# A decoder's second layer: two batches' sums of expert results as small parts of their own, and the queries' rotation in two pieces

## The chip, the core and the metric

The kernel runs on one core of a Trainium2 chip. The metric is the time on the device in microseconds, the median of the runs. A core has a matmul engine (TensorE, here PE), a vector engine (VectorE, DVE), a scalar engine (ScalarE, ACT), a general one (GpSimd, POOL) and a queue for transfers (SyncE, SP). Each engine works through its own list of instructions in order and waits for the others by semaphores.

## The reference, cut to what matters

Everything is float32. Four batches (b) of 256 tokens with 256 features go through two layers, each with three blocks, and every block ends with a residual sum and a layer norm:

```python
x = ln(x + attn0(x))                 # layer 0
x = ln(x + state_space(ctx, x))
x = ln(x + experts(x))               # 64 experts, the best 6 of each token, and a shared one
x = ln(x + linear_attention(x))      # layer 1
x = ln(x + cross_attention(x, ctx))  # 32 heads of 8, queries and keys rotated by position
x = ln(x + squared_relu_mlp(x))      # hidden size 1024, rounded to 255 steps of its row's maximum
```

The second layer's blocks start from the weighted sum of the six expert results of a token: `x += w[j] * y[j]`, j from 0 to 5, ahead of the third norm.

## The kernel before

`Net.l0` computes the first layer and leaves the expert results as rows in device memory (`ys`). `Net.tail` computes the rest, and only it concerns us. The 1024 tokens are eight tiles of 128 rows; batch b has the tiles 2b and 2b+1.

The order of the work in `tail` is written by hand, by means of generators. A `Part` wraps a generator; `go()` runs it to its next `yield`, `to(n)` until n yields are done, and `over` says that it has ended. Between two yields stands a piece. No instruction moves on an engine after that: what a piece issues stands in each engine's list in the order of the calls. The parts are, for each batch b:

- `linear(b)`: the sums of the expert results (`sums`, line 1317: one multiply-add of 128x256 on DVE for each of six results of each of two tiles; the results come as tiles `got` by DMA, three buffers, the next load issued by `load_got` after a tile's last product), moments and norm, `turn` (transposition `xtp` to `xT`), then linear attention (`q1p`, `kv1p`, `kvp`, `o1p`, `project` with `prt` and `prp`, a norm, another `turn`).
- `keys(b)` and `queries(b)`: the projection (`kv2p`, `q2p`), a copy to `raw` by ACT, the rotation `rope` into `pad`, and four pieces that each transpose a quarter (`pt`) and copy it to `kT` or `qT`. In `rope` POOL forms two products for each of the two tiles, and four more operations a tile run on DVE (on POOL for keys with b > 0). In `queries` and in `turned` a few matmuls into a scratch bank (`idle`) stand ahead of the first transposition.
- `output(b, oT)`: transpositions `pto`, division by the sums, `project`, norm and `turn`.
- `squared(b, i)`, one for each tile: `ph`, relu by ACT and square by POOL (`hr`); maximum (`xm`, line 1478), and scaling and rounding of `hr` (lines 1482 and 1483) by DVE; transpositions `fpt`; `fpo`, residual and moments; norm and the output's DMA.

The backbone is a loop over k from 0 to 37. Step k computes logits twice: `lgq` for the head group s = k % 8 of batch k // 8, with queries on the partitions, of which DVE takes the maximum (line 1430), and five steps later (`LAG`) `lgk` of the same group, with keys on the partitions, of which ACT takes the exponential (line 1434); `values` multiplies these with the values (`po`, line 1438). The maxima of four steps are transposed (`pm`) by `place`, and their negatives go by DMA as a row into `qT`, which `lgk` reads (`qT<-mxT`). Each step has two halves, and after each half the loop calls `fill(k, n)`, which lets up to n parts run one piece, three from step 5 on:

```python
now = [e for e in todo if not e[0].over and e[1](k)]
now = sorted(now, key=lambda e: e[0] not in soon)[:n]
```

Each entry of `todo` is a part with a condition (`may`): `lin[b]` may run when `lin[b - 1]` is over, `qs[b]` when `lin[b]` and `ks[b]` are over and its rows of the buffer are free, the parts of `sq` once `outs[b]` is over, in an order fixed by the yields that their predecessors have made. At the start of each batch's steps the loop forces what that batch needs (`lin[b].to(99)`, `ks[b].to(99)`, `qs[b].to(3 + s // 2)`).

All short-lived matmul results but `lgk` and `po`, that is `lgq`, `pt`, `xtp`, `q1p` and so on, share one tag of four PSUM banks that are handed out in turn (`bank`). So the n-th of them waits until the (n-4)-th has been read.

Of the kernel before, what the change touches and what calls it, by code (L numbers as in the profile page):

```python
# [61 lines left out]
class Net:  # L62
# [1102 lines left out]
    def tail(self):  # L1165
# [10 lines left out]
        nc, tc = self.nc, self.tc  # L1176
        H, HD, HP, K, NH, LAG = 32, 8, 32, self.K6, 1024, 5
        SCALE = float(np.float32(1.0) / np.sqrt(np.float32(HD)))
        w = self.w
        with ExitStack() as ctx:  # L1180
# [36 lines left out]
            def rope(b, raw, eng):  # L1217

                r = raw.rearrange("p t (h f i) -> p t h f i", h=H, i=2)
                dst = pad[:, :, :, 0:HD].rearrange("p t h (f i) -> p t h f i", i=2)  # L1220
                tmp = p1.tile([P, 2, 2, H, 4], F32, name="rtmp")
                for t in range(2):
                    cs = slice(8 * b + 4 * t, 8 * b + 4 * t + 4)
                    cos, sin = (v[:, cs].unsqueeze(1).to_broadcast([P, H, 4]) for v in self.trig)
                    x1, x2 = r[:, t, :, :, 0], r[:, t, :, :, 1]
                    d1, d2 = dst[:, t, :, :, 0], dst[:, t, :, :, 1]
                    nc.gpsimd.tensor_mul(tmp[:, t, 0], x2, sin)
                    nc.gpsimd.tensor_mul(tmp[:, t, 1], x2, cos)
                    eng.tensor_mul(d1, x1, cos)
                    eng.tensor_mul(d2, x1, sin)  # L1230
                    eng.tensor_sub(d1, d1, tmp[:, t, 0])
                    eng.tensor_add(d2, d2, tmp[:, t, 1])

            def turned(dst, g, n=0):

# [10 lines left out]
            def keys(b):  # L1246
                raw = p1.tile([P, 2, D], F32, name="raw")
                for t in range(2):
                    ps = bank("kv2p", 2 * D)
                    l0 = b * S + t * P  # L1250
                    self.mm(ps, [(w["ctxT"][:, 0, l0:l0 + P], w["wkv2"][:, 0, :])])
                    nc.scalar.copy(raw[:, t, :], ps[:, :D])
                    nc.scalar.copy(vps[b % 3][:, t, :, 0:HD], ps[:, D:].rearrange("p (h d) -> p h d", d=HD))
                yield
                rope(b, raw, nc.gpsimd if b else nc.vector)
                if b < 2:
                    clear(b + 1, nc.gpsimd)
                yield
                for g in range(4):
                    turned(kTs[b % 2], g, (8 if b == 0 else 3) if g == 0 else 0)  # L1260
                    yield

            def queries(b):
                raw = p1.tile([P, 2, D], F32, name="raw")
                ps = bank("q2p", 2, D)
                for t in range(2):
                    self.mm(ps[:, t, :], [(self.xT[b][:, k, t * P:(t + 1) * P], w["wq2"][:, k, :]) for k in range(KD)])
                nc.scalar.copy(raw, ps)
                yield
                rope(b, raw, nc.vector)  # L1270
                yield
                for g in range(4):
                    turned(qTs[b % 2], g, 5 if g == 0 else 0)
                    yield
# [34 lines left out]
                norm([2 * b, 2 * b + 1], res, mv)  # L1309
                yield  # L1310

            def sums(b):
                for i in range(2):
                    t = 2 * b + i
                    got = gots.pop(t)
                    for j in range(K):
                        nc.vector.scalar_tensor_tensor(  # L1317
                            self.x[t], got[:, j, :], self.wj[:, t, j:j + 1], self.x[t], ALU.mult, ALU.add
                        )
                        if b < 2 and j == 2:  # L1320
                            yield
                    load_got()
                    if i == 0:
                        yield
                res = [self.x[2 * b + i] for i in range(2)]
                mv = self.ln_moments(res)
                yield
                norm([2 * b, 2 * b + 1], res, mv)
                yield
# [136 lines left out]
            def squared(b, i):  # L1466
                t = 2 * b + i
                h = p3.tile([P, NH], F32, tag="g", name="hr")
                for n in range(2):
                    sl = slice(n * 512, n * 512 + 512)  # L1470
                    ph = bank("ph", 512)
                    self.mm(ph, [(self.xT[b][:, k, i * P:(i + 1) * P], w["cfc"][:, k, sl]) for k in range(KD)])
                    nc.scalar.activation(h[:, sl], ph, AF.Relu)  # L1473
                    nc.gpsimd.tensor_mul(h[:, sl], h[:, sl], h[:, sl])  # L1474
                yield
                xm = self.small.tile([P, 1], F32, name="xm")
                iv = self.small.tile([P, 1], F32, name="xiv")
                nc.vector.tensor_reduce(xm, h, AX.X, ALU.max)
                nc.vector.tensor_scalar(xm, xm, EPS, None, ALU.max)
                nc.vector.reciprocal(iv, xm)  # L1480

                nc.vector.tensor_scalar(h, h, iv, 255.0, ALU.mult, ALU.mult)
                nc.vector.tensor_scalar(h, h, MAGIC, MAGIC, ALU.add, ALU.subtract)
                nc.vector.tensor_scalar(xm, xm, 1.0 / 255.0, None, ALU.mult)
                yield
                hT = p3.tile([P, NH // P, P], F32, tag="g", name="hT")
                for q in range(0, NH // P, 4):
                    pt = bank("fpt", 4, P)
                    self.idle(pt[:, 0, :], 4 if t > 5 and q == 0 else 0)
                    for j in range(4):  # L1490
                        nc.tensor.transpose(pt[:, j, :], h[:, (q + j) * P:(q + j + 1) * P], self.ident)
                    nc.scalar.copy(hT[:, q:q + 4, :], pt)
                yield
                po = bank("fpo", D)
                self.mm(po, [(hT[:, j, :], w["cpj"][:, j, :]) for j in range(NH // P)])
                r = p2.tile([P, D], F32, name="rf")
                nc.vector.scalar_tensor_tensor(r, po, xm, self.x[t], ALU.mult, ALU.add)
                mv = self.ln_moments([r])
                yield
                norm([t], [r], mv)  # L1500
                nc.sync.dma_start(out=self.out[t * P:(t + 1) * P, :], in_=self.x[t])
                yield


            ks, qs, lin = ([Part(f(b)) for b in range(B)] for f in (keys, queries, linear))
            sq = [Part(squared(t // 2, t % 2)) for t in range(NT)]
            outs = [None] * B
            ks[0].to(99)
            self.exp_and_log()
            lin[0].to(4)  # L1510
            ks[1].to(2)
            lin[0].to(6)
# [1 line left out]
            first, second, k = lin[0], lin[1], ks[1]  # L1514
            for part in (
                second, second, first, second, first, k, first, k, first, first, second, first, k, second, first,
                second, k, first, second, first, second, first, second, first, qs[0], second, qs[0], second, qs[0],
            ):
                part.go()
            assert first.n == 17, first.n  # L1520
            first.to(99)
            ks[1].to(99)
            qs[0].to(3)

            def may(b):

                def rows(n, k):
                    return b < 2 or k >= 8 * (b - 2) + (3 + 2 * n if n > 1 else 6)  # L1530

                yield lin[b], lambda k: b == 0 or lin[b - 1].over
                yield ks[b], lambda k: b == 0 or (qs[b - 1].over and rows(ks[b].n, k))
                yield qs[b], lambda k: lin[b].over and ks[b].over and rows(qs[b].n, k)
                for i in range(2):
                    p, t = sq[2 * b + i], 2 * b + i
                    yield p, lambda k, p=p, t=t: (
                        outs[b] and outs[b].over and lin[-1].n > 1 and (t < 1 or sq[t - 1].n)
                        and (t < 2 or sq[t - 2].over) and (b == 0 or sq[2 * b - 1].n > (2 if p.n < 2 else 4))
                    )  # L1540

            todo = [e for b in range(B) for e in may(b)]

            def fill(k, n):

                soon = [p[min(k // 8 + 1, B - 1)] for p in (lin, ks, qs)]
                now = [e for e in todo if not e[0].over and e[1](k)]
                now = sorted(now, key=lambda e: e[0] not in soon)[:n]
# [7 lines left out]
            for k in range(8 * B + LAG + 1):  # L1556
                mt = divmod(k, 8) if k < 8 * B else None
                wt = divmod(k - LAG, 8) if 0 <= k - LAG < 8 * B else None
                if mt:
                    b, s = mt  # L1560
                    if s == 0:
                        lin[b].to(99)
                        ks[b].to(99)
                        mxs[b] = p2.tile([P, 2, 2, 16], F32, name="mx2")
                    qs[b].to(3 + s // 2)
                ws = [None] * 4
                for i in range(2):
                    half(i, wt, mt, ws)
# [152 lines left out]
```

## Time and profile before

| | before |
|---|---|
| median of 3 runs | 1191.1 us (1188.24 to 1193.07) |
| profiled execution: its own time | 1182.05 us |
| its span, first to last instruction | 1179.9 us |
| mean granted PE clock | 0.945 |
| PE busy | 1041.2 us (88%), 6340 matmuls |
| PE's weight loads | 764.2 us (65%) |
| DVE busy | 754.4 us (64%), 1572 instructions |
| ACT busy | 431.2 us (37%) |
| POOL busy | 343.9 us (29%) |

`tail` begins at about 805 us of the span; the step k = 0 begins at about 854 us. From 850 to 1180 us PE is busy 296 of 330 us. "Idle before" an instruction is the time for which its engine had nothing to run, and what stands behind the arrow is what ended it. PEclk is the clock that the chip granted to PE, 1.00 or 0.50 at any one moment; a mean over a stretch lies between. Times of single rows are from the one profiled execution, the median is from other executions of the same program.

### The profile page before, as it was taken

The page shows a single profiled execution, that of the slowest core. Times are in us where ns is not written, and L with a number is a line of the kernel's source. Part 1 is how long each engine was busy: PE and PEld are TensorE (multiplying, and loading weights), DVE is VectorE, ACT ScalarE, POOL GpSimd, SP SyncE. Part 2 cuts the span into 40 slices and gives each one's busy share as a digit, 9 for nine tenths or more (in the row PEclk, how much of TensorE's full clock was granted, in tenths as well). Part 3 has the DMA queues.
Part 4 walks back from the last instruction along what each step waited for, and adds up shares of the span by engine and source line. Part 5 has one row for each costly group of instructions (what it writes and reads, how often), then busy time and mean ns, then how long its engine had stood idle before and what let it go on. Part 6 is the DMA issues. An engine that isn't in the chain of part 4 may idle for free.

```text
span 1179.9 us, 17067 instructions
## 1 busy us (share of the span) xinstructions
PE 1041.2 (88%) x6340; PEld 764.2 (65%) x6340; DVE 754.4 (64%) x1572; ACT 431.2 (37%) x809; POOL 343.9 (29%) x593
## 2 busy tenths in 40 slices
PE   6899898899999998897579988897789989899996
PEld 5567574676767675766479977786665655655564
DVE  1647776687879788867546666646667664656433
ACT  2453444435353534333102222123314525444532
POOL 0013323213333332444634645336101212101001
PEclk9899998899999999998789999998968979989999
DMA  8104426265737263222958989954100000000000
GB/s 272 56 1 138 115 45 173 63 200 154 205 97 192 61 173 79 54 73 75 322 189 245 293 242 282 272 178 153 54 1 29 2 1 1 2 11 5 8 9 9
DMA packets 85052, 133.82 MB, mean 113 GB/s; under 512 B 10618, under 2 KB 58896, under 8 KB 84963
## 3 DMA queue, kind: packets, MB, share of 16 engines
q1 hardware_dynamic: 69539, 98.74, 27.8%
q0 software_dynamic: 11008, 31.74, 11.1%
q10 hardware_dynamic: 4416, 2.18, 0.7%
q8 instruction: 52, 0.85, 0.3%
q14 instruction: 37, 0.30, 0.1%
HBM read 86.76 MB, written 31.58 MB: 100 GB/s over the span
## 4 chain that ended last, share of the span: by engine, by line
PE 29%; DMA 10%; DVE 7%; ACT 2%; POOL 1%; issue 1%; SPq 0%; ACTq 0%; DVEq 0%
PE lgk L101 4%; PE gv L101 4%; DMA xg<-xs 4%; DMA wg<-in_L_ffn_wg 3%; PE py L101 3%; PE fpo L101 2%; PE po L1438 2%; PE ph L101 2%; PE lgq L101 2%; DVE x L1317 1%; PE prp L101 1%; PE pt L1241 1%; DVE mx L1430 1%; DMA wk<-in_L_attn_wkT 1%; DMA wv<-in_L_ffn_wv 1%
## 5 line engine op out<-in xcount | busy, mean ns | idle before, releaser
L1430 DVE TENSOR_REDUCE mx<-lgq 128x2 f32<-128x512 f32 x128 | 81.9, 684 | 54.8 <-PE lgq L101 54.8
L958 POOL DMA_INDIRECT ys<-y,to x68 | 69.8, 1026 | 105.3 <-ACT y L1132 96.2
L386 DVE TENSOR_TENSOR_SCAN h<-dA,h 128x512 f32<-128x512 f32 x64 | 96.3, 1504 | 4.3 <-POOL dA L367 4.3
L1434 ACT ACTIVATE w<-lgk 128x512 f32<-128x512 f32 x128 | 69.6, 595 | 78.9 <-PE lgq L101 53.3
L259 DVE TENSOR_TENSOR at<-ps_at,c 128x384 f32<-128x384 f32 x128 | 63.7, 550 | 47.3 <-PE ps_at L101 46.5
L101 PE MATMUL lgq<-kT,qT 32*128 32x256 f32 x512 | 84.4, 458 | 3.9 <-ACT qT L1244 2.0
L101 PE MATMUL lgk<-qT,kT 32*128 32x256 f32 x512 | 83.0, 431 | 4.0 <-DMA qT<-mxT 3.7
L989 ACT ACTIVATE h<-gv 128x176 f32<-128x176 f32 x76 | 24.1, 318 | 160.4 <-PE gv L101 142.3
L365 POOL TENSOR_TENSOR h<-du,bc 128x512 f32<-128x512 f32 x64 | 81.1, 1271 | 0.0
L101 PE MATMUL po<-v,at 128*128 128x128 f32 x384 | 53.0, 291 | 17.7 <-DVE at L259 15.3
L101 PEld LDWEIGHTS po<-v,at 128*128 128x128 f32 x384 | 48.5, 201 | 30.2 <-DVE at L259 16.8
L990 DVE TENSOR_TENSOR h<-h,gv 128x176 f32<-128x176 f32 x76 | 25.6, 337 | 65.0 <-ACT h L989 64.7
L101 PEld LDWEIGHTS lgk<-qT,kT 32*128 32x128 f32 x512 | 49.2, 198 | 26.7 <-issue 17.0
L101 PE MATMUL vg<-wv,xT 128*128 128x512 f32 x128 | 60.5, 627 | 5.4 <-ACT ET L495 4.7
L101 PE MATMUL py<-wo,hT 88*128 88x256 f32 x272 | 64.4, 379 | 0.8 <-ACT y L1132 0.8
L101 PE MATMUL vg<-wg,xT 128*128 128x512 f32 x128 | 58.4, 599 | 0.0
L101 PEld LDWEIGHTS lgq<-kT,qT 32*128 32x128 f32 x512 | 51.4, 212 | 9.7 <-ACT qT L1244 4.2
L1474 POOL TENSOR_TENSOR hr<-hr 128x512 f32<-128x512 f32 x16 | 17.6, 1100 | 133.2 <-ACT hr L1473 133.2
L877 POOL DMA_INDIRECT xs<-xp,rows x48 | 48.4, 1008 | 26.7 <-issue 13.3
L101 PEld LDWEIGHTS py<-wo,hT 88*128 88x128 f32 x272 | 50.2, 190 | 6.5 <-ACT y L1132 1.1
L364 POOL COPY apart<-at 1x1 f32<-1x1 f32 x26 | 5.4, 209 | 167.3 <-DVE at L259 167.3
L101 PE MATMUL gv<-wg,xgT 128*128 128x176 f32 x272 | 51.9, 313 | 0.0
(382 smaller groups left out, 2369.4 us busy)
## 6 DMA issues: line engine op xcount, KB each, us to landing
bc<-bc SPq DMA_DIRECT2D x32, 512.0 KB
y<-h POOLq DMA_DIRECT2D x32, 512.0 KB, 5.1
xs<-none SPq DMA_DIRECT2D x27, 528.0 KB
wg<-in_L_ffn_wg SPq DMA_DIRECT2D x32, 352.0 KB
wv<-in_L_ffn_wv SPq DMA_DIRECT2D x32, 352.0 KB
wo<-in_L_ffn_wo SPq DMA_DIRECT2D x32, 352.0 KB
xg<-xs SPq DMA_DIRECT2D x34, 264.0 KB
got<-ys SPq DMA_DIRECT2D x8, 768.0 KB
```

Source lines behind the costliest of these rows:

```text
L101: self.nc.tensor.matmul(out, lhsT=l, rhs=r, start=i == 0, stop=i == n - 1)
L259: nc.vector.tensor_mul(sb[z], ps[z], self.mask)
L365: nc.gpsimd.tensor_mul(st["hs"][i // 2][:, c, :], du[hf][c], st["bcs"][i // 2][:, 0, :])
L386: nc.vector.tensor_tensor_scan(h, st["dAs"][i], h, 0.0, ALU.mult, ALU.add)
L877: put = nc.gpsimd.indirect_dma_start(out=self.xs, out_offset=bass.IndirectOffsetOnAxis(ap=idx, axis=0), in_=row, in_offset=None,)
L958: put = nc.gpsimd.indirect_dma_start(out=ys, out_offset=bass.IndirectOffsetOnAxis(ap=to[:, i:i + 1], axis=0), in_=y[:, i, :], in_offset=No ...
L989: nc.scalar.activation(h_i, g_i, AF.Silu)
L990: nc.vector.tensor_mul(h_i, h_i, v_i)
L1430: nc.vector.tensor_reduce(mxs[b][:, s // 4, :, 4 * j + s % 4], lg, AX.X, ALU.max)
L1434: nc.scalar.activation(ws[j], lg, AF.Exp, scale=SCALE)
L1438: nc.tensor.matmul(po[j * HP:(j + 1) * HP, s % 2, :], lhsT=vps[b % 3][:, kc, 4 * s + j, :], rhs=ws[j][:, kc, :], start=kc == 0, stop=kc == 1,)
L1474: nc.gpsimd.tensor_mul(h[:, sl], h[:, sl], h[:, sl])
```

## The change

It concerns the order of the work in `tail`, and six things in it:

1. `products(b, n)` is a generator of its own for the sums, with a yield after every n products. For batches 0 and 1, `sums` runs it with n = 3 inside `linear`, as before. For batches 2 and 3 it becomes a part of its own (`rest`) with n = 2, and `sums` starts with the moments.
2. `fill` runs one piece of the first unfinished part of `rest` ahead of its other pieces, at every call from step 6 on (`k > LAG`), beyond the n pieces that it lets run otherwise. `lin[2]` and `lin[3]` may begin when the part of `rest` of their batch is over; it is forced with the rest at the start of the batch's steps. Before, two pieces of `lin[b]` held six products each, the second with the moments.
3. `rope` yields between its two tiles where DVE does it, so that queries have one piece more, and the numbers in the conditions rise by one.
4. `squared` yields between the maximum and the scaling for the tiles 0 to 5. The conditions of `sq` count one yield more, and ask for `rest[-1].over` in place of `lin[-1].n > 1`.
5. The load of ACT's table (`exp_and_log`) is issued after the first piece of `ks[0]` in place of its last.
6. In the hand-written list ahead of the loop, `qs[0]` stands twice in a row for the two pieces of the rotation.

The core of the diff:

```diff
             def rope(b, raw, eng):
...
                     eng.tensor_add(d2, d2, tmp[:, t, 1])
+                    if t == 0 and eng is nc.vector:
+                        yield
...
-            def sums(b):
+            def products(b, n):
+
                 for i in range(2):
                     t = 2 * b + i
                     got = gots.pop(t)
...
-                        if b < 2 and j == 2:
+                        if j == K - 1:
+                            load_got()
+                        if j % n == n - 1 and (i, j) != (1, K - 1):
                             yield
-                    load_got()
-                    if i == 0:
-                        yield
+
+            def sums(b):
+                if b < 2:
+                    yield from products(b, 3)
                 res = [self.x[2 * b + i] for i in range(2)]
...
                 nc.vector.reciprocal(iv, xm)
+                if t < 6:
+                    yield
 
                 nc.vector.tensor_scalar(h, h, iv, 255.0, ALU.mult, ALU.mult)
...
+            ks[0].to(1)
+            self.exp_and_log()
             ks[0].to(99)
-            self.exp_and_log()
...
+            rest = [Part(products(b, 2)) for b in (2, 3)]
...
-                yield lin[b], lambda k: b == 0 or lin[b - 1].over
+                yield lin[b], lambda k: b == 0 or (lin[b - 1].over and (b < 2 or rest[b - 2].over))
                 yield ks[b], lambda k: b == 0 or (qs[b - 1].over and rows(ks[b].n, k))
-                yield qs[b], lambda k: lin[b].over and ks[b].over and rows(qs[b].n, k)
+                yield qs[b], lambda k: lin[b].over and ks[b].over and rows(qs[b].n - 1, k)
...
-                        outs[b] and outs[b].over and lin[-1].n > 1 and (t < 1 or sq[t - 1].n)
-                        and (t < 2 or sq[t - 2].over) and (b == 0 or sq[2 * b - 1].n > (2 if p.n < 2 else 4))
+                        outs[b] and outs[b].over and rest[-1].over and (t < 1 or sq[t - 1].n)
+                        and (t < 2 or sq[t - 2].over)
+                        and (b == 0 or sq[2 * b - 1].n > (3 if p.n < (3 if t < 6 else 2) else 5))
...
             def fill(k, n):
 
+                for e in [e for e in rest if not e.over][:k > LAG]:
+                    e.go()
...
                     if s == 0:
+                        if b > 1:
+                            rest[b - 2].to(99)
                         lin[b].to(99)
                         ks[b].to(99)
...
-                    qs[b].to(3 + s // 2)
+                    qs[b].to(4 + s // 2)
```

With that the pieces land as follows (k.i is the half i of step k): batch 2's products in the fills of 6.0 to 8.1 (before 6.0 and 6.1), batch 3's in 9.0 to 11.1 (before 14.0 and 14.1); the rotation of queries 1 in 6.1 and 7.0 (before 6.1 alone), its first transposition in 7.1 (before 7.0); the later pieces of `linear(2)` and `linear(3)` two to four halves further back; the first pieces of `squared` of batches 1 and 2 at most one half further back.

More of the change, by code (lines that the diff above doesn't have):

```diff
@@ L1254, in keys @@
                 yield
-                rope(b, raw, nc.gpsimd if b else nc.vector)
+                yield from rope(b, raw, nc.gpsimd if b else nc.vector)
                 if b < 2:
@@ L1269, in queries @@
                 yield
-                rope(b, raw, nc.vector)
+                yield from rope(b, raw, nc.vector)
                 yield
@@ L1516, in tail @@
                 second, second, first, second, first, k, first, k, first, first, second, first, k, second, first,
-                second, k, first, second, first, second, first, second, first, qs[0], second, qs[0], second, qs[0],
+                second, k, first, second, first, second, first, second, first, qs[0], second, qs[0], qs[0], second, qs[0],
             ):
@@ L1522, in tail @@
             ks[1].to(99)
-            qs[0].to(3)
+            qs[0].to(4)
+            rest = [Part(products(b, 2)) for b in (2, 3)]
             def may(b):
```

## The prediction

> **What bounds the kernel now.** I read the page's slices first: PE is busy in nearly all of them, so only PE's idle time and its clock can give anything back. Then the waits of PE, the timeline around the longest, and the stretches in which the granted clock was low. The diff touches the last 370 us alone. From 855 us on PE waits for these (engine, waited-for, total us, times, longest):
>
> ```profile
> PE fpt L1491 <- DVE xm L1484: 4.8, 4, 1.6
> PE pt L1241 <- DVE pad L1232: 4.5, 4, 1.8
> PE lgk L101 <- DMA qT<-mxT: 3.7, 3, 1.8
> PE pt L1241 <- POOL pad L1232: 2.2, 2, 1.9
> PE pt L1241 <- DVE mx L1430: 1.7, 1, 1.7
> PE lgq L101 <- DVE mx L1430: 1.1, 1, 1.1
> ```
>
> The two waits for `mx` belong to the products that the diff cuts up. In the timeline (start, us, engine, line) six products and the moments stand ahead of the reductions that free the logits' banks, and PE's transposition has to wait for such a bank:
>
> ```profile
> 895.27 3.08 DVE L1317 SCALAR_TENSOR_TENSOR x<-got,wj,x 128x256 f32<-128x256 f32 x6
> 898.27 0.42 DVE L113 BATCH_NORM_STATS2 ln_st<-x 128x6 f32<-128x256 f32 x1
> ...
> 899.35 1.25 DVE L1430 TENSOR_REDUCE mx<-lgq 128x2 f32<-128x512 f32 x2
> ...
> 900.06 1.12 PE L1241 MATMUL pt<-c,pad 128*128 128x128 f32 x4 [1.74 <-DVE mx L1430]
> ...
> 945.93 3.08 DVE L1317 SCALAR_TENSOR_TENSOR x<-got,wj,x 128x256 f32<-128x256 f32 x6
> 948.93 1.28 DVE L1430 TENSOR_REDUCE mx<-lgq 128x2 f32<-128x512 f32 x2
> ...
> 949.67 1.08 PE L101 MATMUL lgq<-kT,qT 32*128 32x256 f32 x3 [1.13 <-DVE mx L1430]
> ```
>
> After both waits the clock is halved. The view of stretches (us; busy us of PE, PEld, DVE, ACT, POOL; then the clock) shows it:
>
> ```profile
> core 0: us, PE busy (x) PEld busy (x) DVE busy (x) ACT busy (x) POOL busy (x), PEclk, DMA share, GB/s
> 886.11:899.76 13.65, 11.93 (x122) 7.12 (x117) 12.49 (x31) 5.81 (x11) 1.84 (x4) 1.00 0.19 59
> 899.76:906.59 6.83, 6.53 (x35) 3.88 (x36) 4.29 (x9) 3.81 (x8) 1.45 (x3) 0.50 0.00 0
> 950.96:961.20 10.24, 10.24 (x51) 5.96 (x47) 7.07 (x17) 3.81 (x8) 0.00 (x0) 0.50 0.00 0
> 968.03:974.86 6.83, 6.83 (x33) 3.83 (x32) 1.61 (x3) 1.56 (x3) 0.00 (x0) 0.50 0.01 4
> 1005.58:1008.99 3.41, 3.41 (x19) 3.08 (x23) 1.91 (x8) 0.59 (x1) 0.00 (x0) 0.50 0.00 0
> 1049.95:1056.78 6.83, 6.79 (x48) 3.56 (x50) 2.34 (x5) 2.15 (x7) 0.00 (x0) 0.50 0.01 2
> ```
>
> A stretch at 0.50 in which PE is busy loses half its length, so a wait of 1.1 us cost 6.2 in all. DVE was busy 12.49 of 13.65 us before the first drop.
>
> **The change, part by part.** I call a half of step k "k.i". Set beside each other engine by engine, the two programs hold the same PE and DVE work; places differ. From rows at full clock: a bare half takes PE 1.80 us (892.14 to 893.94); DVE needs 1.29 for its two reductions, 1.03 for two products, 0.82 for the rotation of one tile, 1.08 for moments, 0.72 for a norm's two writes.
>
> *Batch 2's products and queries 1.* The products now run in 6.0 to 8.1, batch 3's in 9.0 to 11.1, two ahead of each fill. In 6.1 and 7.0 DVE has 1.29 + 1.03 + 0.82 = 3.14 against PE's 1.80; from 6.1 to 9.1 it has 20.1 against some 16.7, so PE can lose up to 3.4 and at best nothing. Following both queues and the four shared banks half by half: the first transposition of queries 1 (7.1) waits 0.85 for the second tile's rotation, 8.0 waits 0.35 for ACT's copy, 9.0 0.1 for the row DMA, 9.1 0.3 for a bank, and batch 2's transposition 0.75 for the norm: 2.35, which I take. Away go 1.74 and half of 6.83: **+2.8**.
>
> *Batch 3's products* leave 14.0 and 14.1. There DVE then has at most 4.1 (reductions, residual with moments, two reciprocals with their products) against PE's 4.6; no new wait comes out. 1.13 and half of 10.24 go: **+6.25**.
>
> *Queries 2 (15.1).* The residual's matmuls now come before the queries', so DVE does residual and moments (1.75) while PE does the queries (1.85); only ACT's copy stands before the rotation. PE's gaps become about 1.0 and 0.85 for 1.77 and 0.68: **+0.6**. The clock's fall after them I keep.
>
> *Queries 3 (23.1)* no longer have residual and moments ahead: gaps 0.5 and 0.8 for 1.59 and 0.48, **+0.75**; of two half-speed windows after them I take one away, **+1.7** (bounds 0 and 3.4).
>
> *Keys 3.* POOL's rotation took 5.46, with two of its operations at 0.86 and 0.90 instead of 0.41 while DVE scaled `hr` beside it. The scaling moves a half later, so twelve times 0.41 = 4.9; and PE comes 0.85 later, with k and v of batch 3 (1.9) in place of `kvp` (1.05). The wait of 1.88 falls to 0.5 and with it the half-speed window: 1.4 + 1.7 = **+3.1**. With the cover gone it stays 1.88.
>
> *Batch 3's later pieces* move two to four halves back; waits of 0.66 and 0.19 there become 0.3 (bounds 0 and 0.85): **+0.5**.
>
> *The square's rounding as a piece of its own* delays the transposition by a half. Batch 0: 0.60 + 0.48 go, 0.45 comes at 20.0 (0.72 and 1.55 of DVE work in 19.1): **+0.6**. Batch 1: the other tile's maximum (1.5) now stands ahead of the first tile's scaling, and a reduction waits behind it. From the end of the second `ph`: squares 1.8 to 1.9 later, reduction and maximum to 3.85, scaling to 5.4, while PE arrives at 3.5: a wait of 1.9. Against it go 1.33 (`xm`) and 1.05 (row DMA at 1091, now behind two `fpo` of 3.6): **+0.45**. Batch 2 has no reductions by then: scaling to 4.85, PE at 3.4, wait 1.45 for 0.77: **-0.7**. The end of the program follows that one.
>
> *With one answer.* The table load (1.28) moves into ACT's idle 3.39 us ahead of 812.81; the next wait of PE (821.93) ends on DVE's chain, so nothing either way, at most 1.28 if that idle time were gone. The last `got` load is issued near 897 instead of 892.57; DMA was busy 0.78 and 0.09 in the two slices from 894 us on, its first product is due near 918, and the row DMA behind it on SP is issued near 902: free. Output writes change places with row DMAs on SP (0.34 us each), nobody waits.
>
> *New half-speed windows.* Places: 7.1 to 8.0, and the waits of 1.9 and 1.45. In the rows, windows of 3.41 us with PE busy 1.04, 1.47, 1.53, 1.71 and 1.93 were followed by 0.50, also one with 2.28; ones with 2.00 to 2.18 were not, nor was one with 1.57. Bounds: none, or two at each place (10.2). I take two: **-3.4**.
>
> Sum: 2.8 + 6.25 + 0.6 + 0.75 + 1.7 + 3.1 + 0.5 + 0.6 + 0.45 - 0.7 - 3.4 = 12.6 us. The profiled execution took 1182.05 (span 1179.9): 1169.4 by its own measure. It lay 9 us below the median of the runs, 1191.1, so the forecast for the median is 1178.5.
>
> **Rivals.** *Only the gaps go.* The clock might fall for another reason and stay as often low. Without every clock term: -0.6 + 1.13 + 0.6 + 0.75 + 1.4 + 0.5 + 0.6 + 0.45 - 0.7 = 4.1 us, 1187. Against it: five falls each follow a gap of 1.1 us or more, and DVE's blocks stand before two of them. [...] Chance 0.17.
>
> *All clock falls of the edited places go*: 12.6 + 3.4 + 3.4 (queries 2) + 1.7 (the other window of queries 3) = 21, 1170. For it: a gap that a window's edge splits costs nothing. Chance 0.20.
>
> *Slower: DVE paces PE and the clock stays low.* Where DVE has 3.14 against 1.80, and at the two waits behind the other tile's maximum, PE might idle in each window, as from 855.39 on, when five windows in a row ran at 0.50 (17.07 us). Five at each of three places cost 25.6 against 14.35 + 1.7: 1200. It decides from thirteen windows on (22 us of loss, slower by 0.5%). Against it: at 0.50 PE is the slower one again and fills its windows, as in the rows above. Chance 0.08.
>
> That the products still stand in blocks is excluded by the order: never more than two between reductions.
>
> **Numbers.** Forecast 0.55, the rest as given. The range takes in both faster rivals' values and nearly all of the forecast's clock bounds: 1168.5 to 1190. About 0.5% (6 us) can be told from no change; below 1185.1: 0.55 x 0.9 + 0.20 and a little of the first rival, 0.71; within: 0.21; slower: 0.08.
>
> **What would show it.** The profile after should have no wait of PE for `mx` over 1 us at the products, full clock where 950.96 to 961.20 was low, waits near 0.8 at queries 1, about 0.5 at keys 3, about 1.9 and 1.45 at the transpositions of batches 1 and 2. I am wrong if half-speed stretches from 886 us on add up to as much as before (34 us), or if PE waits more than 5 us between 6.1 and 9.1.

## Result and profile after

The change makes the kernel faster: 1174.5 us (median of 16 executions, 1162.8 to 1183.8) against 1187.0 us (median of 16, 1176.6 to 1194.6), a ratio of 0.988 with a 95% interval of 0.9841 to 0.9919, that is 10 to 19 us. Ratios and intervals here rest on the executions within 1.5% of the shortest of their kernel (10 of these 16; 5 of 12 of the kernel without the rotation's piece), while means and their ± are over all executions. By the means the change saves 11.2 ± 2.3 us (1175.0 against 1186.2). The forecast was 12.6 us less and a median of 1178.5.

The profiled execution of after took 1176.98 us (span 1174.8), 5.1 us less than that of before. The place that the change touches gained more. From the first logits of half 6.0 to the end before needed 293.0 us and after 281.1, so 11.9 us less; ahead of it after lost 6.8 us, of which 1.7 ahead of the first `kv2p`. From there to 6.0 its two profiles take 87.0 us, the three of before 79.5 to 82.0, nearly all by the clock: at full clock that is 66.6 us against 66.6 to 70.3. The kernel with the products alone, which up to 6.0 is the same as before, takes 85.6. So this part moves by several us without any change.

The view of PE's waits of after, from 856 us on (engine, waited-for, total us, times, longest):

```profile
PE pt L1243 <- DVE pad L1232: 5.7, 7, 1.2
PE fpt L1499 <- DVE xm L1492: 4.7, 3, 2.0
PE lgk L101 <- DMA qT<-mxT: 2.6, 3, 1.3
...
PE kvp L101 <- DVE mx L1436: 1.5, 2, 0.8
...
PE fpt L1499 <- DVE hr L1491: 1.4, 1, 1.4
```

Both waits of `pt` and `lgq` for `mx` are gone, and so is the one for POOL at keys 3; the wait of `fpt` for `hr` is new. The timeline (start, us, engine, line) at queries 1, where the blocks of six stood:

```profile
901.46 1.28 DVE L1436 TENSOR_REDUCE mx<-lgq 128x2 f32<-128x512 f32 x2
...
902.66 0.99 DVE L1320 SCALAR_TENSOR_TENSOR x<-got,wj,x 128x256 f32<-128x256 f32 x2
...
904.52 0.55 PE L1243 MATMUL pt<-c,pad 128*128 128x128 f32 x3 [0.58 <-DVE pad L1232]
```

Two products stand between reductions, and PE waits 0.58 us, for the second tile's rotation. A stretch at 0.50 is called a fall of the clock below. The stretches of after (us; busy PE, PEld, DVE, ACT, POOL; clock):

```profile
897.30:913.32 16.02, 15.39 (x175) 9.07 (x174) 14.11 (x35) 9.62 (x19) 1.47 (x4) 1.00 0.17 53
963.53:970.36 6.83, 6.83 (x45) 3.85 (x47) 2.64 (x8) 2.65 (x6) 0.00 (x0) 0.50 0.01 3
1100.06:1106.89 6.83, 6.83 (x32) 2.96 (x29) 0.00 (x0) 2.83 (x5) 0.00 (x0) 0.50 0.01 2
1120.54:1127.37 6.83, 6.83 (x32) 4.62 (x31) 0.77 (x3) 3.92 (x7) 0.00 (x0) 0.50 0.00 0
```

From the first logits of 6.1 to those of 9.1 (first row) the clock is full, PE is busy 15.39 and DVE 14.11 of 16.02 us. The other three rows are all that is halved from step 6 on, 20.5 us against 34.4.

Two measures are used below. The list of results gives each execution's span and mean granted clock. Twice the missing clock times the span is the **low time**; the span times the clock is the **length at full clock**. The latter is approximate: half of every halved stretch counts as lost. Where PE is busy the rows bear that out (four transpositions `pt` took 1.12 us at 0.50, at 900.06 us of before, and 0.60 at 1.00, at 829.95); that idle time is lengthened too is not shown. In the 16 executions of after the low time goes from 93 to 163 us, and the span follows it (correlation 0.93). So most of what differs between these executions is how long the clock was halved.

| kernel | ratio to before (95%) | length at full clock, us | low time, us |
|---|---|---|---|
| before (35) | 1 | 1116.0 ± 0.8 | 138 ± 3 |
| after (16) | 0.988 (0.9841 to 0.9919) | 1108.3 ± 0.9 | 129 ± 5 |
| products alone (12) | 0.9959 (0.9912 to 1.0006) | 1111.4 ± 0.7 | 136 ± 4 |
| without products (12) | 1.0046 (1.0004 to 1.0088) | 1115.1 ± 1.3 | 145 ± 3 |
| without the rounding's piece (12) | 0.9965 (0.9927 to 1.0003) | 1111.3 ± 1.0 | 134 ± 4 |
| without the rotation's piece (12) | 0.9923 (0.9881 to 0.9966) | 1105.3 ± 1.0 | 136 ± 4 |
| before, second series (11) | 1 | 1116.0 ± 1.0 | 145 ± 3 |
| table load back (6) | 0.9861 (0.9812 to 0.9911) | 1108.0 ± 1.7 | 125 ± 5 |
| earlier tile first (6) | 0.9898 (0.9848 to 0.9947) | 1108.2 ± 2.6 | 132 ± 6 |
| filled gaps (6) | 0.9829 (0.977 to 0.9888) | 1111.4 ± 1.2 | 114 ± 5 |
| one rotation, earlier tile first (6) | 0.9811 (0.9751 to 0.987) | 1103.9 ± 2.3 | 130 ± 9 |
| before, third series (11) | 1 | 1116.9 ± 1.2 | 164 ± 5 |
| after again (6) | 0.9865 (0.9814 to 0.9917) | 1109.8 ± 2.1 | 146 ± 7 |
| combined (6) | 0.9814 (0.9768 to 0.986) | 1112.8 ± 0.7 | 126 ± 2 |

In brackets is the number of executions; ± is the standard error of the mean over all of them. Products alone to without the rotation's piece are one series, with the 35 executions of before; after itself was timed earlier, beside the 16 of before above. Each series ran on one chip, so low times are best compared within a series.

### The profile page after: what moved, and what is told of

It reads as the page before. It is cut to its first block, busy times and chain, and to the rows that moved or that the text cites. A ratio compares the mean times of both kernels' runs of the same rounds, so it can differ in the third digit from the quotient of the medians.

```text
span 1174.8 us, 17071 instructions
## 1 busy us (share of the span) xinstructions
PE 1041.4 (89%) x6340; PEld 764.0 (65%) x6340; DVE 753.7 (64%) x1572; ACT 430.8 (37%) x809; POOL 341.7 (29%) x593
## 3 DMA queue, kind: packets, MB, share of 16 engines
q0 software_dynamic: 11008, 31.74, 11.1%
## 4 chain that ended last, share of the span: by engine, by line
PE 55%; DVE 21%; DMA 12%; POOL 4%; ACT 4%; issue 3%; ACTq 0%; SPq 0%; POOLq 0%; DVEq 0%
DVE h L386 5%; PE lgk L101 5%; PE po L101 4%; PE qk L101 4%; DMA xg<-xs 4%; PE gv L101 4%; PE vg L101 4%; PE ps_at L101 3%; DMA wg<-in_L_ffn_wg 3%; POOL xs L877 3%; PE ok L101 3%; PE po L1444 3%; PE py L101 3%; PE fpo L101 2%; PE ph L101 2%
## 5 line engine op out<-in xcount | busy, mean ns | idle before, releaser
L101 PE MATMUL lgq<-kT,qT 32*128 32x256 f32 x512 | 79.0, 446 | 2.1 <-ACT qT L1246 2.0
L1291 POOL TENSOR_TENSOR x<-x,bo 128x256 f32<-128x256 f32 x16 | 11.9, 766 | 147.2 <-PE xtp L1287 147.2
L101 PEld LDWEIGHTS lgq<-kT,qT 32*128 32x128 f32 x512 | 48.9, 207 | 6.5 <-ACT qT L1246 4.2
L101 PE MATMUL gv<-wv,xgT 128*128 128x176 f32 x272 | 52.6, 317 | 0.0
```

What stands on the lines that cost most here:

```text
L101: self.nc.tensor.matmul(out, lhsT=l, rhs=r, start=i == 0, stop=i == n - 1)
L1291: nc.gpsimd.tensor_add(self.x[2 * b + j], self.x[2 * b + j], bias)
```

## The experiments

**Products alone.** The change's products part in the kernel before, with rotation, rounding and table load as they were:

```diff
+            def products(b, n):          # as in the change
+            rest = [Part(products(b, 2)) for b in (2, 3)]
+                for e in [e for e in rest if not e.over][:k > LAG]:
+                    e.go()
```

> The kernel before with the products of batches 2 and 3 as parts of their own and nothing else (rotation and rounding in one piece, the table load where it was). My theory (the blocks of six products make PE wait at 900 and 949.67 us, and a wait of over 1 us halves the clock after it): both blocks' terms, 1.74 + 3.4 and 1.13 + 5.1, less some 2.4 of new gaps at queries 1, a gain of about 9 us, a ratio to the kernel before of 0.992 (0.990 to 0.995). Rival 1 (only the gaps go, the clock falls anyway): 0.5 us of 1187, 0.9995. Rival 2 (the gain of the whole change comes from the rounding's and the rotation's new places): 1.000.

Measured 0.9959, with the interval from 0.9912 to 1.0006: it holds both my 0.992 and rival 1's 0.9995. The means (5.9 ± 2.3 us less) and the length at full clock (4.6 ± 1.1 less) show a gain of some us, but the low time, 136 against 138, shows no fall of its own. The trace says more. From 6.0 to the end it lasts 282.8 us, 9.0 less than the mean of three profiles of before (291.8, below), as I had expected; 17.3 us of that are halved, against 26.5 to 34.4, a difference in the clock that the low time of its twelve executions does not bear out. From 6.0 to 9.0 no wait over 0.2 us is left, and from 6.0 to 974 us no halved stretch; both of those I had claimed for the products. A wait of 0.62 for POOL is new at 10.1. And a larger one comes later, which eats part of the gain. With the products gone, the pieces behind them come earlier, and at batch 0's squares DVE does a tile's maximum and scaling in one go (timeline):

```profile
1008.55 1.21 DVE L1482 TENSOR_REDUCE xm<-hr 128x1 f32<-128x1024 f32 x1
...
1011.64 1.28 DVE L1434 TENSOR_REDUCE mx<-lgq 128x2 f32<-128x512 f32 x2
...
1012.38 0.66 PE L1494 MATMUL fpt<-c,hr 128*128 128x128 f32 x4 [1.90 <-DVE mx L1434]
```

The second `fpt` needs a bank that only the reduction at 1011.64 frees, and that stands behind 3.1 us of squares: 1.90 us, and 0.75 for `lgq` just before. Keys 3's wait for POOL, 1.88 in before, is 0.15 here.

**Without products.** The rest of the change, with the sums of all batches inside `linear`:

```diff
-            def products(b, n):
-            rest = [Part(products(b, 2)) for b in (2, 3)]
+                        if b < 2 and j == 2:
+                            yield
+                    load_got()
+                    if i == 0:
+                        yield
```

> The kernel after with the sums of all batches inside the linear parts again (blocks of six for batches 2 and 3); the rotation and the rounding in two pieces and the table load stay. My theory: the products' share of the forecast, 2.8 + 6.25 of 12.6 us, is gone, and what is left is 3 to 4 us, a ratio to the kernel before of 0.997; if the table load's new place costs the 3.4 us that the profile after shows between 804 and 852 us, 1.000. Rival (the rounding and the rotation carry the gain): 0.988 to 0.990 as the whole change.

Measured 1.0046 (1.0004 to 1.0088). Over all executions the means are 1189.5 ± 1.6 and 1187.2 ± 1.2 us, and at full clock it is 0.9 us shorter than before, so that it is slower is not shown; but no gain is left. That denies the rival clearly, and my 3 to 4 us of remaining gain too: from 6.0 to the end its profile lasts 291.4 us, as before. The timeline shows one reason:

```profile
903.13 3.20 DVE L1319 SCALAR_TENSOR_TENSOR x<-got,wj,x 128x256 f32<-128x256 f32 x6
...
908.26 3.08 DVE L1319 SCALAR_TENSOR_TENSOR x<-got,wj,x 128x256 f32<-128x256 f32 x6
...
913.05 1.37 PE L101 MATMUL pt<-c 128*128 128x128 f32 x7 [3.53 <-DVE mx L1432]
```

With the rotation in two pieces one tile's rotation stands between the two blocks and the other behind the second, and the reduction at 912.33 frees PE's bank only then: a wait of 3.53 where before had 1.74. Beside blocks of six the other two edits bring nothing that is seen; what they do for after, they do only together with the products.

**Without the rounding's piece.**

```diff
                 nc.vector.reciprocal(iv, xm)
-                if t < 6:
-                    yield
```

> The kernel after with the maximum and the scaling of the squares in one piece again. My theory: by the sum the piece gave 0.6 + 0.45 - 0.7, the wait of keys 3 with its window 3.1, and cost two new half-speed windows, 3.4: nothing in all, a ratio to the kernel before of 0.988 as the whole change (0.986 to 0.990). The profile should show again a wait for POOL at keys 3 near 1.9 us and waits at the transpositions of batches 1 and 2 near 1.3 and 0.8 us in place of 2.00 and 1.42. Rival (the waits of 2.00 and 1.42 us with their windows are the dearest thing left): 0.984.

Measured 0.9965 (0.9927 to 1.0003), and 3.0 ± 1.3 us more at full clock than after; neither 0.988 nor 0.984 lies in the interval. The waits of 1.33 and 0.77 us at tiles 2 and 4 came back as expected. Keys 3 did not: there is no wait for POOL over 0.2 us, but the 1.90 and 0.75 us of the products alone. And queries 3 wait 1.59 + 0.48 as in before, where after waits 0.72 + 0.68. So beside the products the piece is worth something, not nothing. How much is less sure: 5.5 ± 2.4 us by the means, 1180.5 and 1175.0, which come from two series, and 1.9 by the profiles from 6.0 to the end (281.4 against a mean of 279.5 for two of after).

**Without the rotation's piece.**

```diff
-                    if t == 0 and eng is nc.vector:
-                        yield
...
-                yield from rope(b, raw, nc.vector)
+                rope(b, raw, nc.vector)
```

> The kernel after with the rotation of the queries in one piece again. My theory: 6.1 then holds both tiles' rotation on top of two products and two reductions, 4.0 us of DVE against 1.80 of PE, so the first transposition of queries 1 waits 1.6 us or more and the clock may fall once; and queries 2 and 3 lose their new order, 0.6 + 0.75 + 1.7: 3 to 5 us slower than the whole change, a ratio to the kernel before of 0.991 to 0.992. Rival (DVE's order inside those halves does not matter, since PE has work queued): 0.988.

Measured 0.9923 (0.9881 to 0.9966), which would fit my 0.991 to 0.992. But over all twelve executions, one of them unusually short (1158.5 us), the mean is 1175.2 us against 1175.0 for after, and the length at full clock is 3.0 ± 1.3 us less: a loss of 3 to 5 us is not shown. The trace denies its reason. From 6.0 to 9.0 it has no wait of PE over 0.2 us, where after has 0.58; 0.61 comes at 10.1 instead. Queries 2 and 3 wait 1.16 + 0.69 and 0.72 + 0.68 us, as in after to 0.01. The reordered queries come from the other two edits; of the rotation's piece no use is shown, and from 6.0 to the end the profile without it is 2 us shorter at full clock (269.0 against 270.8 and 271.1).

**Table load back.**

```diff
-            ks[0].to(1)
-            self.exp_and_log()
             ks[0].to(99)
+            self.exp_and_log()
```

> The kernel after with ACT's table load where it was, behind the last piece of the first keys. The forecast put it at nothing. Theory A (nothing either way): a ratio to the kernel before of 0.990 as the whole change (its 16 runs had a mean of 1175.0 against 1186.2), and a stretch from the first kv2p to step 0 of the same length at full clock, 46 to 47 us. Theory B (it costs, because POOL's rotation and its memset of 1.80 us now fall on DVE's products and norm: 6.48 for 6.14 and 1.96 for 1.04 us in the profile after): the stretch is 1.3 us shorter, and the ratio 0.987 to 0.989.

The ratio, 0.9861 (0.9812 to 0.9911), does not tell the two apart; the stretch does. From the first `kv2p` to step 0 it is 47.6 us at full clock with the load back, 46.7 in both profiles of after, and 45.4, 47.4 and 45.2 in three profiles of before. Theory B falls: the load's place costs nothing that is seen among differences of 2 us.

**Earlier tile first.** Where one fill holds pieces of two tiles' squares, the earlier tile's is run first:

```diff
+                at = [i for i, e in enumerate(now) if e[0] in sq]
+                own = list(now)
+                for i, e in zip(at, sorted((now[i] for i in at), key=lambda e: sq.index(e[0]))):
+                    own[i] = e
-                for e in now:
+                for e in own:
                     e[0].go()
```

> The kernel after; where one fill runs pieces of two tiles' squares, the earlier tile's comes first, so that the scaling of tile 2 (and 4) stands ahead of the maximum of tile 3 (and 5) on DVE. My theory: the waits of 2.00 and 1.42 us fall by the 1.5 us of that maximum to 0.5 and nothing, and with the second its two half-speed windows (1120.54 to 1127.37): 2.9 + 3.4 us less, a ratio to the kernel before of 0.984 to 0.986. Rival (the wait moves on to the second tile's transposition, as PE has nothing to do in between): waits for xm of 1 to 2 us a half later, ratio 0.989 to 0.990 as the whole change.

The timeline shows the first part of my theory:

```profile
1059.68 0.15 DVE L1492 TENSOR_SCALAR xm<-xm 128x1 f32<-128x1 f32 x1
1059.74 1.21 DVE L1484 TENSOR_REDUCE xm<-hr 128x1 f32<-128x1024 f32 x1
...
1059.91 1.06 PE L1499 MATMUL fpt<-c,hr 128*128 128x128 f32 x8 [0.49 <-DVE xm L1492]
...
1061.26 1.27 DVE L1436 TENSOR_REDUCE mx<-lgq 128x2 f32<-128x512 f32 x2
...
1061.98 0.48 PE L101 MATMUL lgq<-kT,qT 32*128 32x256 f32 x1 [0.38 <-DVE mx L1436]
```

The wait of 2.00 is 0.49 and the one of 1.42 is gone; so the order of the two tiles on DVE was their cause, as the prediction had it. The time does not follow as expected: 0.9898 (0.9848 to 0.9947). From 6.0 to the end the length at full clock is 269.4 us against 270.8, so 1.4 of the 2.9 us, and that is tile 4's share. Tile 2 gives nothing: the halves 27.1 and 28.0 together take 11.56 us, in after 11.52. The reduction at 1061.26 now stands behind the other tile's maximum, and the logits of 28.0 wait for it (0.38 us, and their matmuls come further apart). So at tile 2 the rival is right that the wait moves on, though to the logits and not to the second tile's transposition. In the profile of the table load back, without this edit, the clock did not fall at tile 4 either, so 3.4 us for it was too much. The interval holds after's 0.988: in time nothing is shown against after.

**Filled gaps.** Scratch matmuls in idle time of PE:

```diff
-                    turned(qTs[b % 2], g, 5 if g == 0 else 0)
+                    turned(qTs[b % 2], g, (14 if b == 2 else 5) if g == 0 else 0)
...
+                        if n > 9 and s == 0 and t == 1:
+                            self.idle(pt[:, 1, 1, :], 5)
...
-                    self.idle(pt[:, 0, :], 4 if t > 5 and q == 0 else 0)
+                    self.idle(pt[:, 0, :], {2: 15, 4: 11, 6: 4, 7: 4}.get(t, 0) if q == 0 else 0)
```

> The kernel after with matmuls into scratch in three of PE's idle times: 9 more ahead of the first transposition of queries 2 and 5 between its first and second, 15 ahead of the transpositions of tile 2's squares, 11 ahead of tile 4's (0.12 us each by the rows of such matmuls, 18 in 2.17 us). They shorten no path, they only keep PE busy. If the clock falls because a window of 3.41 us holds too little of PE's work, the falls at queries 2 and at tile 4 are gone in every execution: 3.4 us each where they were, the low time of all executions 129 us less some 10, a ratio to the kernel before of 0.984 to 0.987. Rival (the falls come on their own): low time as before, 129 us, and a ratio of 0.990.

Measured 0.9829 (0.977 to 0.9888), with a low time of 114 ± 5 us, 11 to 18 below the other three of its series. The stretch over queries 2 is at full clock here, where each of the twelve profiles without these fillers has 3.41 us or more halved:

```profile
957.50:970.00 12.50, 12.46 (x122) 9.34 (x121) 8.30 (x25) 6.01 (x14) 1.66 (x4) 1.00 0.01 3
```

At tile 4 the fall is gone too; the one after the wait for the row's DMA, which nothing fills, is there (1099.19, 6.83 us). The kernel combined, below, has the same fillers at queries 2 and no fall there either. At queries 2, then, the fall hangs on how much PE has to do in the gap, and does not come on its own. At tile 4 one profile without fillers has no fall (the table load back), so there nothing follows. The fillers are a little too many: 0.9 us at queries 2, 1.2 us more from 25.0 to 29.0, and 3 us in the length at full clock (1111.4 against 1108.0 with the table load back). That they make the kernel faster than after is not shown by this run alone: its mean is 1170.7 ± 2.7 us, that of the table load back, in the same series, 1172.7 ± 2.1.

**One rotation, earlier tile first.** The edits of "Without the rotation's piece" and "Earlier tile first" together.

> The kernel after with the rotation in one piece again and the earlier tile's squares first. By the runs so far the rotation's two pieces give nothing (means 1175.0 with, 1175.2 without, and without them no wait at queries 1), so this should be as the kernel with the earlier tile first, a ratio to the kernel before of 0.983 to 0.986. Rival (the rotation's second piece is needed where PE comes earlier): 0.988.

Measured 0.9811 (0.9751 to 0.987), and the shortest at full clock, 1103.9 ± 2.3. The interval leaves out the rival's 0.988, and holds my range. By the means, 1171.2 ± 2.9 against 1190.4 ± 1.5 us, the ratio is 0.984, from which 0.988 is not far; and the filled gaps (1170.7) and the table load back (1172.7) of its series are level with it.

**The kernel before, twice more.**

> The kernel before, unchanged, for a second profile. Question: do the half-speed stretches from which I priced the products' blocks come back? My forecast's theory (a wait of over 1 us halves the clock): 6.83 us after the wait near 900 and some 10 us after the one near 950, as in the first profile. Rival (whether a gap halves the clock depends on where the edges of the windows of 3.41 us fall, which differs from execution to execution: of the ten profiles' windows with PE busy 1.4 to 1.8 us about half were followed by 0.50): the waits of 1.74 and 1.13 us are there to 0.05 us, but one or both of the falls are missing or shorter.

> The kernel before, unchanged, for a third profile; the same question and the same two answers.

The waits from which I priced are the same to 0.01 us: 1.74, 1.13, 1.76 + 0.68, 1.88, 1.59 + 0.48. One other is not: tile 0's second is 1.29 in both, 0.48 in the first profile. The stretches of the second profile:

```profile
966.49:973.32 6.83, 6.83 (x34) 4.26 (x34) 6.01 (x15) 2.64 (x7) 0.00 (x0) 0.50 0.00 0
...
1062.07:1065.48 3.41, 3.41 (x23) 1.38 (x24) 1.57 (x3) 1.09 (x2) 0.00 (x0) 0.50 0.00 0
```

Batch 2's block is followed by 6.83 us in all three profiles. Batch 3's has 6.83 in these two, not 10.24; keys 3 none, not 3.41; queries 3 3.41, not 6.83. And the kernel without products has the same 1.13 us wait at 962.11, with no fall after it. So both answers are half right: the falls at the blocks come back, but their lengths, and at other waits their being there, depend on the execution. From 6.0 to the end the three profiles have 34.4, 27.6 and 26.5 us halved and last 293.0, 291.8 and 290.7 us.

**After again, and combined.** The second is one rotation and earlier tile first, with other fillers:

```diff
-                    turned(qTs[b % 2], g, 5 if g == 0 else 0)
+                    turned(qTs[b % 2], g, (14, 5, 14, 11)[b] if g == 0 else 0)
...
-                    self.idle(pt[:, 0, :], 4 if t > 5 and q == 0 else 0)
+                    self.idle(pt[:, 0, :], {2: 4, 6: 14, 7: 10}.get(t, 0) if q == 0 else 0)
```

> The kernel after, unchanged, beside the next one on the same chip and for a second profile. A ratio to the kernel before of 0.986 to 0.990. The waits of 1.16, 0.72, 2.00 and 1.42 us should be the same to 0.05 us; the falls after 1100 us (two of 6.83) need not be there, by the rival of the kernels before.

> The kernel after with the rotation in one piece, the earlier tile's squares first, and scratch matmuls in PE's idle times at the queries of all batches but 1 (9, 9 and 6 more ahead of the first transposition, 5 between the first and the second), 4 at tile 2's squares and 10 and 6 more at the last two tiles'. If an underfilled window is what halves the clock, the falls at queries 0, 2 and 3 and in the last 20 us go or shrink, and the low time of all executions is some 110 us as with the filled gaps (114) or less, with the shorter path of one rotation and earlier tile: a ratio to the kernel before of 0.975 to 0.981. Rival (fillers and order do not add up, since the filled idle time is the same): 0.982.

After repeats: 0.9865 (0.9814 to 0.9917). Its waits but those for the row's DMA are the same to 0.01 us, the fall after tile 4's wait is there, the one at the row's DMA is not. From 6.0 to the end it lasts 277.9 us with 13.7 halved. Combined has 0.9814 (0.9768 to 0.986), and its executions are 6.7 us shorter than after's on the same chip (means 1178.0 ± 0.9 and 1184.7 ± 1.6). Its low time is 126 us against 146, and 164 for before, while at full clock it is not shorter than after (1112.8 against 1109.8): what it gains on after, it gains by the clock. Its profile shows one place of it: where step 0 begins, 3 to 24 us are halved in the 13 other profiles, and none here, where queries 0 have fillers. 0.9814 lies between my upper 0.981 and the rival's 0.982 and does not tell the two apart; 0.975 lies outside the interval. It beats before and after; from one rotation with earlier tile first it cannot be told.

## Why the prediction was right

Direction, size and mechanism held: from 6.0 to the end the mean of the three profiles of before is 291.8 us and that of two of after 279.5, 12.3 less, where the sum said 12.6. That it came so close is in part luck, because two errors cancel: at full clock 6.1 us went (277.1 to 271.0), where the gap terms gave 4.1, and the halved clock gave 6.2, where its terms gave 8.5. The gaps and the clock can be told apart in the pair of profiles that the forecast used. Waits of PE by the prediction's steps:

| place | before | forecast | after |
|---|---|---|---|
| batch 2's block, then queries 1 | 1.74 | 2.35 | 0.58 + 0.23 |
| batch 3's block | 1.13 | 0 | 0 |
| queries 2 | 1.77 + 0.68 | 1.0 + 0.85 | 1.16 + 0.68 |
| batch 3's later pieces | 0.66 + 0.19 | 0.3 | 0.65 |
| keys 3 | 1.88 | 0.5 | 0 |
| tile 0's squares | 0.60 + 0.48 | 0.45 | 0.32 |
| queries 3 | 1.59 + 0.48 | 0.5 + 0.8 | 0.72 + 0.68 |
| tile 2's squares, and the row's DMA | 1.33 + 1.05 | 1.9 | 2.00 |
| tile 4's squares | 0.77 | 1.45 | 1.42 |
| sum | 14.4 | 10.1 | 8.4 |

- *Queries 1* is the term that was mis-sized. I expected DVE to have 20.1 us of work in the seven halves from 6.1 to 9.1, the last included, against 16.7 of PE. The same work, from the reduction at 898.54 to the next step's at 917.92, kept DVE busy 18.63 us, and PE, from 897.30 to 916.09, 17.93. So DVE had 0.7 us more to do than PE, not 3.4, and PE's waits came to 0.81. DVE spends less on a step than the sum of the rows says (the two reductions that take 1.29 by their row start 1.2 us before what follows), and PE more than I had counted. Three of the five new waits did not appear.
- *Keys 3 and tile 0* came out better than forecast, by an exchange that I had not seen. I had put keys 3's gain down to the rounding's piece; but with the products alone the wait is 0.15, and in after without that piece there is none. The products bring keys 3 clear of POOL, and put a wait of 1.90 us at tile 0, which the rounding's piece takes away.
- *The new waits* of 2.00 and 1.42 us came within 0.1 of the forecast. Waits for the row's DMA of 0.47 at 938.62 and 0.75 at 1099.70 (0.88 in before) were not in my sum.
- *The clock.* I gave back two halved windows for new waits and kept one at queries 3. After has four new ones (two behind the row's DMA, two behind tile 4's wait; in its second profile only the latter) and none at queries 3. At queries 2 the fall stayed, as forecast, and at both blocks and keys 3 it is gone. In the pair the halved time went from 34.4 to 20.5 us, 6.9 us of time where the sum had 8.5; the repeats give (29.5 - 17.1) / 2 = 6.2.
- *The rivals.* "Only the gaps go" is denied: the low time falls with the change (on one chip 164 to 146 us, on another 145 to 125 with the table load back), and so do the halved stretches from 6.0 on (26.5 to 34.4 us in three profiles, 20.5 and 13.7 in two). "All clock falls go", 1170, needed the fall at queries 2 gone, and it is there in both profiles. "DVE paces PE" is denied by PE's 15.39 busy of 16.02 us at full clock.

Two grounds were weaker than the result. I priced clock falls from one execution: 10.24, 3.41 and 6.83 us at three places were 6.83, 0 and 3.41 in two other profiles. And I credited parts one by one, 9.05 of the 12.6 us to the products. From 6.0 to the end at full clock before lasts 275.8 to 278.0 us, a mean of 277.1; the products alone have 274.1, the rest without them 278.5, and the whole change 271.0. The parts are no sum: 3.0 us and nothing make 6.1 together. By the means of the executions (5.9 ± 2.3 less, 2.3 ± 2.0 more, 11.2 ± 2.3 less) it looks the same, at the edge of the noise.

## What to carry to other kernels

When a vector engine's block delays the reductions that free a matmul's banks, cut the block to what the slack of one step holds; then follow every later piece, because it moves up and may meet the next block, which has to be cut too. Price a halved clock from several executions or by how full each window is, and where an idle time cannot be removed, try scratch matmuls in it (here the filled gaps had a low time of 114 us, the other three of their series 125 to 132). Undo each part of a combined change by itself: here one of three showed no use, and another was worth something only beside the third. And when a wait is gone, look whether the half behind it became longer.

## What the runs showed of the hardware

In the profiles of before and after the granted clock takes the values 1.00 and 0.50 alone, and all its changes (37 and 41) lie within 1 ns of a grid of 3413.33 ns, fitted to each. The grid does not follow the program: its first edge comes 2.1 us after the first instruction in the profile of before, 0.5 us in the second profile of the same kernel (by its stretches from 915.29 to 1065.48 us), and 1.0 us in after. So a wait of the same length can be cut by the edges in different ways. The clearest case is tile 2's wait of 2.0 us, in two kernels that do the same there. After and the kernel with the table load back, two windows each (clock behind POOL's busy time):

```profile
1062.52:1065.93 3.41, 2.03 (x28) 1.10 (x24) 3.31 (x7) 2.32 (x5) 0.27 (x1) 1.00 0.00 0
1065.93:1069.34 3.41, 2.79 (x33) 2.01 (x34) 3.38 (x8) 1.65 (x4) 0.00 (x0) 1.00 0.00 0
```

```profile
1058.17:1061.58 3.41, 1.42 (x19) 1.22 (x19) 3.31 (x9) 1.60 (x4) 0.00 (x0) 1.00 0.00 0
1061.58:1064.99 3.41, 3.41 (x27) 1.52 (x21) 2.79 (x6) 1.47 (x3) 0.00 (x0) 0.50 0.00 0
```

The same wait is cut into windows with 2.03 and 2.79 us of PE's work, and the clock stays; or it falls whole into one, with 1.42, and the next window is halved. Over the windows at full clock in the profiles of before and after, from 10 us after the start on: of those with PE busy below 1.4 us all 18 were followed by 0.50; from 1.4 to 1.8 us 10 of 22; from 1.8 to 2.8 us 9 of 96; above that 2 of 468. What tells the middle ones apart is open.
